# Layer 1's scores computed for two heads at a time, from keys and queries that are no longer stacked

## The chip, the core and the metric

The kernel runs on one core of a Trainium2 chip. TensorE multiplies matrices out of SBUF into PSUM, VectorE (DVE), ScalarE (ACT) and GpSimd (POOL) do the elementwise work, and SyncE (SP) issues nearly all DMAs, which share 16 DMA engines. The metric is the device time of one execution in microseconds. Before the change three runs took 1598.06, 1599.79 and 1607.69 us, with a median of 1599.79 us.

## The reference

Two layers of cross attention work on 8 batches. Each batch has 100 queries and a context of 722 rows, all 512 wide. Layer 0 has 16 heads of 32 features, layer norms and a feed forward of 2048. Layer 1, cut to what matters here, is:

```python
qh = (q @ Wq).reshape(b, sq, H, DK)            # H = 16 heads, DK = 64
kh = (k @ Wk).reshape(b, sk, H, DK)            # sk = 722
vh = (v @ Wv).reshape(b, sk, H, DV)
attn = jnp.einsum('bqhd,bkhd->bhqk', qh / jnp.sqrt(jnp.float32(DK)), kh)
weights = jax.nn.softmax(attn + gaussian_w, axis=-1)
out = jnp.einsum('bhqk,bkhd->bqhd', weights, vh).reshape(b, sq, H * DV)
out = layernorm(out @ Wfc + residual)
```

A score is thus a sum over 64 features, while TensorE's array has 128 rows to sum over.

## The kernel before, in words

Float32 numbers are kept as pairs of float16, a high part and a low part, and a product of two such pairs is made of the terms high·high, high·low and low·high (`TERMS`), summed in PSUM.

The work goes by 24 units. Units 0 to 7 are layer 0, one batch each, with 16 heads. Units 8 to 23 are layer 1: a unit is half of a batch's heads, so 8 heads of 64 features. While the heads of one unit are worked on, the keys and values of the next unit are projected (`proj`), and between them run the feed forward, the queries of layer 1 and the output projections.

**Keys.** `proj_k` makes 4 pieces of 128 features (two heads of layer 1) by two halves of 361 keys. Each half is 12 matmuls into a PSUM bank; ACT writes the high part (`nc.scalar.copy`) and DVE the low part into a tile `KN` (2 buffers) whose 128 partitions are the features of two heads. When both halves are done, `stack` makes layer 1's stacked form in a tile of `KSR` (4 tiles, 4 heads each, tile name `ks`): per head, 64 partitions with the high part and 64 with the low part. That takes four DMAs per piece, from SBUF to SBUF. `keys_free` holds back the piece that takes the next `KSR` tile until the heads that last used that tile are on their way.

**Queries.** The queries of layer 1 lie in DRAM (`QD1`). `load_q` brings them in with four DMAs per unit, high and low parts each twice, once for each half of the partitions.

**Scores.** `scores` makes, for one head and each half of 361 keys, two matmuls with 128 rows: the high query part against high and low keys stacked, then the low query part against the same. (So low·low is included.) The result is a tile `S` of two PSUM banks; the pool `ps_s` has two such tiles. DVE takes the maximum over the 722 keys (`nm`). `front1` then scales it (`nb`), makes the exponentials on ACT (`p`), casts them to float16 (`stage`, by ACT or DVE in turns), makes the low part on POOL, and transposes both with a DMA into a tile `pt`. `head_back` multiplies `pt` with `V` in 18 matmuls into `O`.

**What sets the order.** `step(u, h)` writes the scores of head h and then the softmax of the head before it, which waited in `stages`. Between the steps the fill items (`merge`) are written at even rates, each with a cost by hand. In layer 1 `nc.in_order` is empty: the order on each engine is chosen at build time by a planner that simulates the engines and takes, of what is ready, the instruction that stands earliest in the program. Everything in `step` counts as standing 120 instructions earlier than it is written (80 in the last unit). So a head's four score matmuls are planned as single instructions among those of other streams, and need not stay together.

PSUM has 8 banks: 4 for the two `S` tiles, 1 for `O`, and 3 for all projections (`pp` twice and `nzb`).

Of the kernel before, what the change touches and what calls it, by code (L numbers as in the profile page):

```python
# [21 lines left out]
# the products of a split pair: high*high, high*low, low*high  # L22
TERMS = ((0, 0), (0, 1), (1, 0))
# layer 0's rows of outputs: the heads whose products share a bank of PSUM
# [4 lines left out]
class Engine:  # L29
    """an engine whose instructions can be kept in the order in which they are written"""  # L30
# [23 lines left out]
def xattn_kernel(  # L54
# [33 lines left out]
    # resident weights: what layer 0 is done with makes room for layer 1  # L88
# [56 lines left out]
    def pow2_steps(s, inv, u, k, n):  # L145
        """s = 2**e with sqrt(u) * s <= 2**(15 - k), inv = 1 / s"""
        t, t2, V = small(n, I32, "pa"), small(n, I32, "pb"), nc.vector
        return [
            lambda: V.tensor_single_scalar(t, u.bitcast(I32), 1, ALU.logical_shift_right),
            lambda: V.tensor_scalar(t2, t, -1, 0x5F30F379, ALU.mult, ALU.add),  # L150
            lambda: V.tensor_single_scalar(t, t2, 0x7F800000, ALU.bitwise_and),
            lambda: V.tensor_scalar(s, t.bitcast(F32), 2.0 ** (15 - k), None, ALU.mult),
            lambda: V.tensor_scalar(inv.bitcast(I32), s.bitcast(I32), -1, 254 << 23, ALU.mult, ALU.add)]
# [5 lines left out]
    def rsqrt_steps(v, eps, n, p=128, scale=1.0):  # L159
        """scale / sqrt(v + eps), by Newton's method: the steps and the result"""  # L160
        a, i, yi = small(n, tag="ra"), small(n, I32, "ri"), small(n, I32, "ry")
        V = nc.vector
        l = [lambda: V.tensor_scalar(a[:p], v, eps, None, ALU.add),
             lambda: V.tensor_single_scalar(i[:p], a[:p].bitcast(I32), 1, ALU.logical_shift_right),
             lambda: V.tensor_scalar(yi[:p], i[:p], -1, 0x5F3759DF, ALU.mult, ALU.add),
             lambda: V.tensor_scalar(a[:p], a[:p], -0.5, None, ALU.mult)]
        y = yi.bitcast(F32)
        for it in range(3):
            t, y2 = small(n, tag="rt"), small(n, tag="rz")
            if n == 1:  # L170
                l.append(lambda t=t, y=y: V.tensor_scalar(t[:p], y[:p], y[:p], a[:p], ALU.mult, ALU.mult))
            else:
                l += [lambda t=t, y=y: V.tensor_tensor(t[:p], y[:p], y[:p], ALU.mult),
                      lambda t=t: V.tensor_tensor(t[:p], t[:p], a[:p], ALU.mult)]
            l.append(lambda t=t, y=y, y2=y2: V.scalar_tensor_tensor(y2[:p], t[:p], 1.5, y[:p], ALU.add, ALU.mult))
            y = y2
        if scale != 1.0:
            l.append(lambda: V.tensor_scalar(y[:p], y[:p], scale, None, ALU.mult))
        return l, y
# [7 lines left out]
    def colsum(src, n, p=128):  # L187
        """sums over the partitions, on every partition, in PSUM"""
        ps = psum_misc()
        nc.tensor.matmul(out=ps[:, :n], lhsT=ones[:p, :], rhs=src, start=True, stop=True)  # L190
        return ps[:, :n]
# [8 lines left out]
    XS = 4.0  # scale of what a layer norm returns: at most sqrt(512)  # L200

# [1 line left out]
    # blocks of 256 columns or 256 rows, each with its scale and the inverse; wo has one scale  # L203
# [3 lines left out]
    def weighted_rows(raw, c, acc):  # L207
        """sum over kc of raw[:, kc, :] * c[:, kc], by partition"""
        nc.vector.tensor_scalar(acc, raw[:, 0, :], c[:, 0:1], None, ALU.mult)
        for kc in range(1, KC):  # L210
            nc.vector.scalar_tensor_tensor(acc, raw[:, kc, :], c[:, kc : kc + 1], acc, ALU.mult, ALU.add)
        return acc

    def bias_part(ps, raw, bcol, ocs):
        """ps[:, oc] = sum over rows of raw[row, oc] * bcol[row]"""
# [6 lines left out]
    # -- layer 0: wq, wk, wv, with the gain and shift of the layer norm folded in  # L222
# [30 lines left out]
    # |g| + |b|: with it the sum of squares of a weight bounds what its product with a normed row, shift  # L253
    # included, can be
# [31 lines left out]
    def scale_steps(i, name):  # L286
        """the scale of a weight of layer 0"""
# [26 lines left out]
    # -- DRAM scratch  # L314
# [76 lines left out]
    def first_load():  # L391
        """the context of batch 0, the queries of batches 0 and 1, the weights of layer 0"""
# [81 lines left out]
    def v_tile(u, s):  # L474
        """V of half the heads of a unit: [lo | hi | 1] by head in layer 0, [hi | lo] in layer 1"""
# [11 lines left out]
    def proj_v0(u):  # L487
        L, b, hf = unit_of(u)

        def pair(s, c):  # L490
            """two chunks of keys for half the heads"""
# [52 lines left out]
    def load_q(u, oc=None):  # L544
# [9 lines left out]
        else:  # L554
            q = pool.tile([128, 16, SQ], F16, tag="QS", name="QS").rearrange("p (t h) q -> p t h q", t=2)
            src = QD1.rearrange("(g d) t k -> d g t k", d=64)
            for r in range(2):
                for t in range(2):
                    nc.sync.dma_start(
                        out=q[64 * r : 64 * r + 64, t],  # L560
                        in_=src[:, 8 * hf : 8 * hf + 8, t, b * SQ : (b + 1) * SQ])
# [5 lines left out]
    def keys_free():  # L567
        """whether the heads that use the next tile for a stack of keys are all on their way"""
        return owner.get(counters.get("ks", 0) % len(KSR), None) in used | {None}
# [6 lines left out]
    def proj_k(u):  # L576
# [3 lines left out]
        def piece(oc, j):  # L580
            w = w0["k"] if L == 0 else w1res["k", hf]
            T = ctxT[L, b]
            if j == 0:
                kn[oc] = pool.tile([128, 2, SK], F16, tag="KN", name="KN", bufs=2)
# [18 lines left out]
        def stack(oc):  # L603
# [8 lines left out]
            else:  # L612
                if oc % 2 == 0:
                    KSt[u, oc // 2] = keys_tile(u, 2 * oc + 3)
                KS = KSt[u, oc // 2]
                for j in range(2):
                    for t in range(2):
                        nc.sync.dma_start(
                            out=KS[64 * t : 64 * t + 64, 2 * (oc % 2) + j, :SK], in_=K[64 * j : 64 * j + 64, t, :])
            if u > 0 and oc == (1 if u == LAST else 2 if u < B else 3):  # L620
                load_q(u)
        def item(oc, j):
            f = lambda: piece(oc, j)
            if j == 1 and (L == 0 or oc % 2 == 0):
                f.ready = keys_free
# [8 lines left out]
    def scores(u, h):  # L634
# [3 lines left out]
        for j in range(2):  # L638
            sl = slice(j * HALF, (j + 1) * HALF)
            if L == 0:  # L640
                nc.tensor.matmul(
                    out=S[:SQ, j, :HALF], lhsT=q[:96, h, :], rhs=KS[:96, h % 4, sl], start=True, stop=True)
            else:
                for t in range(2):
                    nc.tensor.matmul(
                        out=S[:SQ, j, :HALF], lhsT=q[:, t, h, :], rhs=KS[:, h % 4, sl], start=(t == 0), stop=(t == 1))
        nm = small(1, tag="nm")
        nc.vector.tensor_reduce(nm[:SQ], S[:SQ, :, :HALF], AX.XY, ALU.max, negate=True)
        return S, nm

    # layer 0: the scores again with the keys on the partitions, less the maximum of each query, which
    # enters the product as two more rows (a power of two by a split pair)
# [105 lines left out]
    def to_T(src, dst, s=None):  # L758
        """split [100, 512] and transpose it into dst [128, 8, 112]"""
# [12 lines left out]
    def o_transposed(u, half=None):  # L772
# [4 lines left out]
        else:  # L777
            # chunks in the order hi 0, hi 1, lo 0, lo 1 | hi 2, hi 3, lo 2, lo 3
# [8 lines left out]
    def project_out(u_list, scr):  # L787
        """[100, 512] = concatenation of the units' outputs times a streamed weight"""
# [152 lines left out]
    ahead = {}  # L941

    def load_ahead():
        """what the ends of the last two batches read"""
# [8 lines left out]
    def out_row(b, ap):  # L953
        """gamma or beta on every partition"""
# [22 lines left out]
    usum = const.tile([128, 8], F32, name="usum")  # L977

    def pipeline(blocks):
        """the steps of the blocks, in an order in which each has the next ones' behind it"""  # L980
# [10 lines left out]
    def block(w, kind, i, col, scr=None, dst=None, total=None, done=None):  # L991
        """kind "rows": rows 256 i up; "cols": columns 256 i up"""
# [70 lines left out]
    def y_scale():  # L1063
        """sy = (scale of what the feed forward's layer norm returns, its inverse, bound of the sum of its squares)"""
# [106 lines left out]
    def merge(lists):  # L1171
        """one list in which the given lists advance at even rates"""
# [224 lines left out]
    def step(u=None, h=None):  # L1397
        """one head further: scores of the next, softmax of the one before, output of an earlier one"""
        with tc.high_priority(offset=80 if u == LAST or u is None and len(pending) and pending[0][0] >= LAST - 1 else 120):
            new = None  # L1400
            if u is not None:
                S, nm = scores(u, h)
                new = (u, h, S, negated(nm) if u < B else nm)
                if u < B:
                    negated_T(u, h, new[3])
# [4 lines left out]
            if new:  # L1410
                stages.append(new)
# [84 lines left out]
```

## Time and profile before

| | |
|---|---|
| runs, us | 1598.06, 1599.79, 1607.69 |
| profiled execution: span, us | 1602.2 (the page gives no other time for it) |
| mean granted TensorE clock | 0.948 of full speed |
| layer 1's part, first score matmul to the end | 712.4 us to 1602.2 us |
| PE busy, whole span | 1390.2 us, 87% |
| DVE, ACT, POOL busy | 66%, 50%, 38% |
| DMA queue of SP | 77.6% of 16 engines' span |

Nearly all instructions carry line L39, that of the helper `Engine.__getattr__` which records every operation. So groups are told apart by their tiles, written as out<-in, with the engine ahead: "PE S<-ks,QS" are the score matmuls, "ACT KN<-pp" the high parts of keys. PEld is the load of a matmul's stationary operand, which overlaps PE. A form such as 128\*100 gives the rows and columns of the array that a matmul uses; 128x361 behind it is what streams through. "busy" is the union of a group's time, then comes the mean duration of one, and then the idle time of the engine just before it with what ended it.

### The profile page before, as it was taken

What the parts mean: (1) busy time and instruction counts of PE and PEld (TensorE: products, weight loads), DVE (VectorE), ACT (ScalarE), POOL (GpSimd) and SP (SyncE); (2) the same over time, 40 slices, a digit from 0 to 9 for tenths busy, and PEclk for the clock granted to TensorE, in tenths of its full rate; (3) what the DMA queues carried; (4) which work ended last, traced back from release to release, by engine and by line L of the source; (5) the groups of instructions that cost most, each with busy time, mean ns of one, the idle gap of its engine ahead of it and who ended that gap; (6) DMA issues with size and microseconds to landing.
All of it is one profiled execution on the core that took longest, in us unless ns stands there. A gap on an engine that the chain in (4) does not pass through costs nothing. (4 is left out here: it accounts for less than half of the span.)

```text
span 1602.2 us, 33216 instructions
## 1 busy us (share of the span) xinstructions
PE 1390.2 (87%) x12394; PEld 973.7 (61%) x12394; DVE 1062.2 (66%) x2761; ACT 797.2 (50%) x1518; POOL 606.0 (38%) x465
## 2 busy tenths in 40 slices
PE   5887888788877989787999889999979999889996
PEld 4665566666656666465666556566556666565674
DVE  6878788888898576785455655455745455545566
ACT  3455656776765566644444334444424443343442
POOL 3234565766764244453222213222313222223341
PEclk9899899898878999999999999999999999999999
DMA  8567789778975595569987689988888976797675
GB/s 200 128 138 182 166 239 207 194 211 199 253 156 137 159 233 169 157 168 187 209 175 176 164 184 205 214 181 176 193 158 200 218 179 168 163 189 161 156 170 112
DMA packets 504019, 289.71 MB, mean 181 GB/s; under 512 B 397054, under 2 KB 435982, under 8 KB 503858
## 3 DMA queue, kind: packets, MB, share of 16 engines
q1 hardware_dynamic: 501714, 287.58, 77.6%
q8 instruction: 97, 1.59, 0.4%
q14 instruction: 64, 0.52, 0.1%
q10 hardware_dynamic: 2112, 0.01, 0.1%
q0 software_dynamic: 32, 0.01, 0.0%
HBM read 149.37 MB, written 35.30 MB: 115 GB/s over the span
## 5 line engine op out<-in xcount | busy, mean ns | idle before, releaser
L39 POOL TENSOR_TENSOR stage<-p,stage 100x722 f16<-100x722 f32 x124 | 196.8, 1590 | 526.4 <-DVE stage L39 250.2
L39 PE MATMUL pp<-wres,ctxT 128*128 128x256 f16 (+3 forms) x1992 | 340.3, 323 | 17.6 <-DVE V L39 12.2
L39 PE MATMUL pp<-ctxT,wres 128*128 128x361 f16 x1800 | 328.0, 332 | 15.0 <-DVE QN L39 6.2
L39 PEld LDWEIGHTS <-wres 128*128 128x128 f16 x2496 | 244.9, 102 | 153.7 <-issue 39.1
L39 PEld LDWEIGHTS <-ctxT 128*128 128x128 f16 (+1 forms) x2376 | 240.9, 105 | 152.1 <-issue 22.1
L39 DVE TENSOR_REDUCE nm<-S 100x1 f32<-100x722 f32 x256 | 229.9, 900 | 67.2 <-PE S L39 66.3
L39 POOL TENSOR_TENSOR pt<-p,pt 128x600 f16<-128x600 f32 x128 | 177.0, 1385 | 168.7 <-ACT pt L39 117.6
L39 PE MATMUL O<-V,pt 128*128 128x64 f16 (+5 forms) x3840 | 193.8, 192 | 28.8 <-DMA pt<-stage 11.2
L39 PEld LDWEIGHTS <-pt 128*128 128x128 f16 (+1 forms) x3840 | 170.6, 99 | 70.6 <-DMA pt<-stage 14.7
L39 PE MATMUL S<-ks,QS 128*100 128x361 f16 (+1 forms) x768 | 186.0, 330 | 30.2 <-issue 8.0
L39 ACT ACTIVATE p<-S,nb,sig 100x722 f32<-100x722 f32 x128 | 121.9, 953 | 156.8 <-DVE nb L39 138.7
L39 ACT CAST V<-pp 128x256 f16<-128x256 f32 (+2 forms) x194 | 78.3, 406 | 121.9 <-DVE V L39 57.4
L39 DVE TENSOR_TENSOR V<-pp,V 128x256 f16<-128x256 f32 (+2 forms) x194 | 89.6, 463 | 63.6 <-ACT V L39 63.4
L39 PEld LDWEIGHTS <-QS 128*100 128x100 f16 (+1 forms) x768 | 91.7, 129 | 61.5 <-issue 29.9
L39 PEld LDWEIGHTS <-wst 128*128 128x128 f16 x1152 | 101.5, 100 | 23.8 <-issue 12.7
L39 ACT ACTIVATE p<-ST,sig 128x600 f32<-128x600 f32 x128 | 97.4, 761 | 27.2 <-PE ST L39 22.7
L39 PE MATMUL nzb<-ctxT,wres 128*128 128x361 f16 x504 | 90.0, 324 | 6.5 <-DVE V L39 2.9
L39 ACT CAST pt<-p 128x600 f16<-128x600 f32 x128 | 87.9, 688 | 2.3
L39 PE MATMUL nzb<-wres,ctxT 128*128 128x512 f16 (+2 forms) x384 | 88.5, 373 | 0.2 <-DVE V L39 0.2
L39 DVE SCALAR_TENSOR_TENSOR hl<-nat,sc,hl 128x512 f16<-128x512 f32 (+1 forms) x48 | 40.8, 851 | 63.5 <-ACT hl L39 63.4
L39 DVE TENSOR_TENSOR KN<-pp,KN 128x361 f16<-128x361 f32 x86 | 45.3, 530 | 54.2 <-ACT KN L39 53.4
L39 PE MATMUL pp<-wst,hT 128*100 128x512 f16 x312 | 76.4, 380 | 2.0 <-DMA wst<-W2S 0.9
(259 smaller groups left out, 2065.6 us busy)
## 6 DMA issues: line engine op xcount, KB each, us to landing
ks<-KN SPq DMA_DIRECT2D x256, 90.2 KB
nat<-in_ctx_dram SPq DMA_DIRECT2D x78, 256.0 KB
ks<-KD SPq DMA_DIRECT2D x96, 180.5 KB
wst<-W1S SPq DMA_DIRECT2D x64, 256.0 KB
wst<-W2S SPq DMA_DIRECT2D x64, 256.0 KB
wst<-WFS SPq DMA_DIRECT2D x48, 256.0 KB
KD<-KN SPq DMA_DIRECT2D x32, 361.0 KB
QS<-QD SPq DMA_DIRECT2D x85, 100.0 KB
```

Of the source, the lines that this page charges most:

```text
L39: r = f(*args, **kwargs)
```

## The change

Layer 1's keys are written by ACT and DVE straight into the `KSR` tile, with the partitions as they come out of the projection: partitions 0 to 63 are one head, 64 to 127 the next, and high and low parts lie side by side. The four stacking DMAs per piece go. Queries are loaded the same way, with two DMAs per unit. The new `scores_pair` makes the scores of two heads together: three terms instead of two stacked products, each a matmul over 64 rows, the first head on rows 0 to 63 and the second on rows 64 to 127, written in turn. It is called at even heads, and takes both `S` tiles. The product low·low is no longer computed. `step` now writes the softmax of the waiting head before the scores. Layer 0 is as before.

```diff
@@ load_q
-            q = pool.tile([128, 16, SQ], F16, tag="QS", name="QS").rearrange("p (t h) q -> p t h q", t=2)
-            src = QD1.rearrange("(g d) t k -> d g t k", d=64)
-            for r in range(2):
-                for t in range(2):
-                    nc.sync.dma_start(
-                        out=q[64 * r : 64 * r + 64, t],
-                        in_=src[:, 8 * hf : 8 * hf + 8, t, b * SQ : (b + 1) * SQ])
+            q = pool.tile([128, 16, SQ], F16, tag="QS", name="QS")[:, :8].rearrange("p (c t) q -> p c t q", t=2)
+            src = QD1.rearrange("(c p) t k -> p c t k", p=128)
+            for t in range(2):
+                nc.sync.dma_start(out=q[:, :, t], in_=src[:, 4 * hf : 4 * hf + 4, t, b * SQ : (b + 1) * SQ])
@@ proj_k, piece
             if j == 0:
-                kn[oc] = pool.tile([128, 2, SK], F16, tag="KN", name="KN", bufs=2)
+                if L == 0:
+                    kn[oc] = pool.tile([128, 2, SK], F16, tag="KN", name="KN", bufs=2)
+                else:
+                    if oc % 2 == 0:
+                        KSt[u, oc // 2] = keys_tile(u, 2 * oc + 3)
+                    kn[oc] = KSt[u, oc // 2][:, 2 * (oc % 2) : 2 * (oc % 2) + 2, :SK]
@@ proj_k, stack and item
-            else:
-                if oc % 2 == 0:
-                    KSt[u, oc // 2] = keys_tile(u, 2 * oc + 3)
-                KS = KSt[u, oc // 2]
-                for j in range(2):
-                    for t in range(2):
-                        nc.sync.dma_start(
-                            out=KS[64 * t : 64 * t + 64, 2 * (oc % 2) + j, :SK], in_=K[64 * j : 64 * j + 64, t, :])
...
-            if j == 1 and (L == 0 or oc % 2 == 0):
+            if j == 1 if L == 0 else j == 0 and oc % 2 == 0:
                 f.ready = keys_free
@@ scores
-            if L == 0:
-                nc.tensor.matmul(
-                    out=S[:SQ, j, :HALF], lhsT=q[:96, h, :], rhs=KS[:96, h % 4, sl], start=True, stop=True)
-            else:
-                for t in range(2):
-                    nc.tensor.matmul(
-                        out=S[:SQ, j, :HALF], lhsT=q[:, t, h, :], rhs=KS[:, h % 4, sl], start=(t == 0), stop=(t == 1))
+            nc.tensor.matmul(
+                out=S[:SQ, j, :HALF], lhsT=q[:96, h, :], rhs=KS[:96, h % 4, sl], start=True, stop=True)
+        return S, maximum(S)
...
+    def scores_pair(u, h):
+        S = [ps_s.tile([128, 2, 512], F32, tag="S", name="S") for _ in range(2)]
+        K, q = KSt[u, h // 4][:, h % 4 : h % 4 + 2], QSt[u]
+        for j in range(2):
+            sl = slice(j * HALF, (j + 1) * HALF)
+            for i, (a, t) in enumerate(TERMS):
+                for r in range(2):
+                    rows = slice(64 * r, 64 * r + 64)
+                    nc.tensor.matmul(
+                        out=S[r][:SQ, j, :HALF], lhsT=q[rows, h // 2, a, :], rhs=K[rows, t, sl],
+                        start=(i == 0), stop=(i == 2))
+        return [(s, maximum(s)) for s in S]
@@ step
-            new = None
-            if u is not None:
+            new = []
+            if u is not None and u < B:
                 S, nm = scores(u, h)
-                new = (u, h, S, negated(nm) if u < B else nm)
-                if u < B:
-                    negated_T(u, h, new[3])
+                new = [(u, h, S, negated(nm))]
+                negated_T(u, h, new[0][3])
             if len(stages) >= (2 if u is not None and u < B else 1):
                 v, g, S_, nm_ = stages.pop(0)
                 pending.append((v, g, front0(v, g, nm_) if v < B else front1(v, g, S_, nm_)))
                 used.add((v, g))
-            if new:
-                stages.append(new)
+            if u is not None and u >= B and h % 2 == 0:
+                new = [(u, h + r, S, nm) for r, (S, nm) in enumerate(scores_pair(u, h))]
+            stages.extend(new)
```

`maximum` is the old code's reduction to `nm`, now a function of its own.

More of the change, by code (lines that the diff above doesn't have):

```diff
@@ L639, in scores, with maximum @@
             sl = slice(j * HALF, (j + 1) * HALF)
-            if L == 0:
-                nc.tensor.matmul(
-                    out=S[:SQ, j, :HALF], lhsT=q[:96, h, :], rhs=KS[:96, h % 4, sl], start=True, stop=True)
-            else:
-                for t in range(2):
-                    nc.tensor.matmul(
-                        out=S[:SQ, j, :HALF], lhsT=q[:, t, h, :], rhs=KS[:, h % 4, sl], start=(t == 0), stop=(t == 1))
+            nc.tensor.matmul(
+                out=S[:SQ, j, :HALF], lhsT=q[:96, h, :], rhs=KS[:96, h % 4, sl], start=True, stop=True)
+        return S, maximum(S)
+    def maximum(S):
         nm = small(1, tag="nm")
         nc.vector.tensor_reduce(nm[:SQ], S[:SQ, :, :HALF], AX.XY, ALU.max, negate=True)
-        return S, nm
+        return nm
+    def scores_pair(u, h):
[10 more added lines that the diff above has]
+        return [(s, maximum(s)) for s in S]
     def negated(nm):
```

## The prediction

> **What bounds the kernel now.** I read the page's busy shares first, then the busy time by stretches, then the groups by form inside layer 1's stretch, then the matmuls in order of time. The first line is the page's, the next two the view by stretches:
>
> ```profile
> PE 1390.2 (87%) x12394; PEld 973.7 (61%) x12394; DVE 1062.2 (66%) x2761; ACT 797.2 (50%) x1518; POOL 606.0 (38%) x465
> ...
> core 0: us, PE busy (x) PEld busy (x) DVE busy (x) ACT busy (x) POOL busy (x), PEclk, DMA share, GB/s
> 712.00:1602.00 890.00, 815.14 (x6824) 535.08 (x6824) 499.47 (x1141) 368.29 (x731) 240.60 (x160) 0.98 0.82 179
> ```
>
> In layer 1 PE is busy 815 of 890 us; the DMA engines come second with 0.82, while DVE and ACT have room. What a change does to PE's stream is therefore nearly what it does to the time. The groups by form, in 712 to 1602 us:
>
> ```profile
> L39 PE MATMUL S<-ks,QS 128*100 128x361 f16 x512 | 119.6, 326 | 13.5 <-issue 8.0 <-DMA ks<-KN 3.4 <-ACT p L39 2.0
> L39 DVE TENSOR_REDUCE nm<-S 100x1 f32<-100x722 f32 x128 | 115.0, 901 | 42.2 <-PE S L39 42.0
> L39 PEld LDWEIGHTS <-wst 128*128 128x128 f16 x900 | 78.1, 99 | 16.4 <-issue 7.1 <-DVE V L39 2.2 <-DVE QN L39 1.4
> L39 PEld LDWEIGHTS <-QS 128*100 128x100 f16 x512 | 63.4, 127 | 39.5 <-issue 12.9 <-DMA ks<-KN 2.4 <-DMA xs<-in_L_xattn_beta_dram 0.7
> L39 ACT CAST KN<-nzb 128x361 f16<-128x361 f32 x42 | 19.3, 460 | 52.9 <-PE nzb L39 32.8 <-DMA ks<-KN 20.1
> ```
>
> A matmul's duration is not its price, since the next starts before it ends. The timeline of PE gives the price, and also shows how the score matmuls of one head stand among the others (two heads here):
>
> ```profile
> 1009.13 0.79 PE L39 MATMUL S<-ks,QS 128*100 128x361 f16 x4 [0.40 <-DMA ks<-KN]
> ...
> 1430.94 0.33 PE L39 MATMUL S<-ks,QS 128*100 128x361 f16 x1 [1.14 <-DMA ks<-KN]
> 1431.11 0.32 PE L39 MATMUL pp<-ctxT,wres 128*128 128x361 f16 x1
> 1431.26 0.32 PE L39 MATMUL S<-ks,QS 128*100 128x361 f16 x1
> 1431.41 0.32 PE L39 MATMUL pp<-ctxT,wres 128*128 128x361 f16 x1
> 1431.57 0.32 PE L39 MATMUL S<-ks,QS 128*100 128x361 f16 x1
> 1431.72 0.32 PE L39 MATMUL pp<-ctxT,wres 128*128 128x361 f16 x1
> 1431.88 0.32 PE L39 MATMUL S<-ks,QS 128*100 128x361 f16 x1
> ```
>
> Four matmuls in 0.79 us, the last of which takes 0.32, start 0.154 to 0.157 us apart: 361 columns cost 0.154. The second head is what matters most here: its matmuls alternate with a projection's. I went through all 128 heads of layer 1 in this view: in 56 the four stand together, in 60 two or three of the three links between them are broken, mostly by one foreign matmul each time. Today that is free, as 0.154 is kept throughout.
>
> **The sum, against the profiled execution's span of 1602.2 us.** The median is 2.4 us lower, inside the runs' spread, so differences are carried over to 1599.8.
>
> *Streams.* Before, two heads take 8 x 0.154 = 1.232 us; 64 pairs are 78.8 us. After, there are 12 matmuls of the same 361 columns. Where both halves of the rows really work at once, the six slots cost 6 x 0.154 = 0.924 us, so 59.1 us in all, a gain of 19.7. Where every matmul runs alone, 12 x 0.154 x 64 = 118.3 us, a loss of 39.5. No matmul of the trace uses half the rows, so these are the bounds. Two matmuls can only run at once if they are neighbours. The two chains of a pair are written in turn and should be ready together (the waits are below), so whole bursts come in the right order, but a stream that stands at the same place in the plan cuts in between. Of the bursts I take 60/128 = 47% as cut. A cut lasts as long as the other chain: 12 or 18 matmuls, entered half way on average, so some 7 of a burst's 11 links. With the odd single cut that is 3.6 broken links per burst, one in three. Six slots then cost 6 x 0.154 x 1.33 = 1.23 us: **0 us**, the gain is eaten by the cuts.
>
> *Changes between half rows and whole rows.* A burst with 3.6 cuts is 4.6 runs, each entered and left: 9.2 changes, 64 x 9.2 = 590. The trace has none, so its price is bounded. Below: nothing, as changes between 96, 98 and 128 rows cost nothing visible. Above: the new matmul waits until the one before has left the array, 0.317 (the median duration of a score matmul) less 0.154 = 0.163 us. I take 0.10, which is nearest to the row of weight loads (99 ns): what today hides beneath the preceding matmul would stand free once per change. That is **+59 us**; the bounds are 0 and +96.
>
> The Trainium skill, "TensorEngine Tiling (Array Packing)", section Tiling Modes (Key Properties), speaks against this change: going from one tiling mode to another, not merely to another tile, drains the engine. No row here shows that; by it the price would lie nearer to the whole tail of a matmul, and the sum nearer to its upper bound. Against that, "TensorE: Matmul & The Clock Gate", Part 3 (Measured speedup vs the span model) gives row tiles that start some 4 ns apart, by which an uncut burst gains nearly all of what the two halves can give; no row here shows that either.
>
> *Weight loads.* 768 in place of 512, 127 ns each as 100 columns; the matmul before hides one. Two per slot, 0.254 us of durations, overlap each other as today's loads do: 0 where they still do so. If they didn't, six slots would lose 0.1 us each, 38 us, no more than the bound of matmuls that run alone.
>
> *DMAs that go.* 256 of 90.2 KB, of which the tile's view shows SP's issue cost:
>
> ```profile
> L39 SPq DMA_DIRECT2D ks<-KN x252: 461/587/1863, 703.6 to 1568.0; - x126
> ```
>
> 252 x 0.587 = 148 us of SP's queue, and by the packet records (15,868 of 1444 bytes, 95 ns each, on 16 engines) 94 us of the engines' 890: their share falls from 0.82 to 0.71. The queries' DMAs fall from 64 to 32. None of it is on the path by itself; the path has PE's idle time that a DMA ended: 27.2 us in layer 1 (`pt` 11.2, `wst` 9.0, `ks` 3.4, `OT` 2.0, smaller ones 1.6). Shorter queues take back a part, between 0 and 27: **-10 us**, the 3.4 and a quarter of the rest. ACT's 29 us of waiting for a free `KN` buffer (20.1 in the last row above) go too, but ACT is idle half the time.
>
> *New waits.* The pair needs both `S` tiles, so its first matmuls stand behind the exponentials of the two heads before; queued behind them on PE is everything else. A pair comes every 890/64 = 13.9 us, and after its scores come two maxima (0.90 each), `nb` (0.24) and two exponentials (0.95 and 0.19 for the sum): some 4.3 us. So 0, with 9 us of cover; without it, up to 4.3 us a pair. DVE's two maxima in a row hold up what stands behind them, the low parts of V and K, by 0.9 us; PE has three banks for projections, and waits 23 us for DVE in layer 1 today. 0, at most 0.9 x 64 = 58 if each delay reached PE. Keys now wait for a free `ks` tile one piece earlier; its last readers are a unit back: 0.
>
> Sum: 0 + 59 - 10 = +49, so **1649 us**.
>
> **The rivals.**
>
> *Faster: the halves work at once and changing costs little.* -19.7 - 10 = -30, **1570 us**, if bursts stay whole and changes are free. For it: 56 of 128 heads stand together today, and both chains of a pair can fill each other's gaps. Against it: the 60 that don't. It decides when streams and changes together cost less than the 10 us from the DMAs: with uncut bursts (128 changes) below 0.23 us a change, with today's cuts below 0.017.
>
> *A wash.* Cuts as today, changes free: 0 - 10, **1590 us**. For it: mixing row counts is free today.
>
> *The halves don't run side by side* (the change doesn't do what it says): +39.5 - 10 = +29, **1629 us**. For it: no matmul of the trace overlaps another's streaming.
>
> *Changing costs the whole tail*: +96 - 10 = +86, **1686 us**.
>
> **Chances and range.** Cut bursts with a change of about a weight load: 0.42. Faster: 0.22. Wash: 0.13. Side by side fails: 0.12. Whole tail, or more cuts than today: 0.11. A measurement of this kernel tells about 1%, 16 us, from no change. That makes 0.22 faster, 0.13 within 1%, 0.65 slower. Cases of both signs hold most of the chance, so the range goes from the faster rival, with some of the DMAs' upper bound, 1566, to the whole tail with part of the two maxima's cost, 1715. The likeliest case's own range is 1612 to 1686.
>
> **What the changed profile would show.** Score matmuls of form 64\*100, 768 of them, whose starts come two at a time if the halves work at once, and 0.154 us apart if not. In the timeline, single score matmuls between foreign ones if the cuts stay, and starts more than 0.154 after a matmul of the other row count if changing costs. No `ks<-KN`, a DMA share near 0.71, PE's idle time behind DMAs below 27 us. "DVE nm" twice in a row, and "PE S" still hardly waiting for "ACT p". I would be wrong if the planner kept bursts whole, or if a change were free; and too low if a weight load could not begin before the array is empty.

## The result: slower by 3.6%, and where the time went

The changed kernel takes 1659.1 us (median of 4 runs, 1651.88 to 1671.47) against 1600.3 us before (median of 4). The ratio is 1.0363, with a 95% interval of 1.0325 to 1.0401. The profiled execution has a span of 1661.8 us, 59.6 us above that of before. Layer 1, from its first score matmul to the end, grew from 889.8 to 948.3 us, by 58.5; so nearly all of it lies there.

The lines that answer to those of before are these: first the page's busy shares, then busy time in layer 1's stretch, then three groups by form in the same stretch.

```profile
PE 1486.2 (89%) x12650; PEld 979.4 (59%) x12650; DVE 1071.5 (64%) x2761; ACT 791.0 (48%) x1518; POOL 606.5 (36%) x465
```

```profile
core 0: us, PE busy (x) PEld busy (x) DVE busy (x) ACT busy (x) POOL busy (x), PEclk, DMA share, GB/s
713.00:1662.00 949.00, 915.20 (x7128) 543.89 (x7125) 508.69 (x1150) 364.22 (x733) 244.28 (x164) 0.98 0.64 140
```

```profile
L39 PE MATMUL S<-ks,QS 64*100 64x361 f16 x768 | 169.1, 339 | 2.7 <-DMA QS<-QD 1.4 <-ACT p L39 1.2
L39 PE MATMUL O<-V,pt 128*128 128x64 f16 x1920 | 110.1, 194 | 5.5 <-DMA pt<-stage 5.5
L39 ACT CAST ks<-pp 128x361 f16<-128x361 f32 x81 | 37.4, 461 | 123.3 <-PE pp L39 123.2
```

PE is busy 96% of layer 1 where it was 92%, and the DMA engines went from 0.82 to 0.64. The score matmuls have the form 64\*100 now, so they do use half the rows. ACT's writing of keys, which had waited 29 us for the stacking DMAs to free `KN`, now waits for nothing but PE. "ACT p" holds up a score matmul for 1.2 us in all: that the pair needs both `S` tiles costs next to nothing.

The timeline of PE shows the price. First a pair that nothing cut, then a stretch of one that was cut at every link:

```profile
958.91 1.14 PE L39 MATMUL S<-ks,QS 64*100 64x361 f16 x12 [0.80 <-DMA QS<-QD]
959.99 0.33 PE L39 MATMUL nzb<-ctxT,wres 128*128 128x361 f16 x1
960.15 0.69 PE L39 MATMUL O<-V,pt 128*128 128x64 f16 x18
...
1534.17 0.28 PE L39 MATMUL O<-V,pt 128*128 128x64 f16 x4
1534.38 0.35 PE L39 MATMUL S<-ks,QS 64*100 64x361 f16 x1
1534.67 0.20 PE L39 MATMUL O<-V,pt 128*128 128x64 f16 x1
1534.80 0.35 PE L39 MATMUL S<-ks,QS 64*100 64x361 f16 x1
1535.09 0.20 PE L39 MATMUL O<-V,pt 128*128 128x64 f16 x1
1535.22 0.35 PE L39 MATMUL S<-ks,QS 64*100 64x361 f16 x1
1535.50 0.20 PE L39 MATMUL O<-V,pt 128*128 128x64 f16 x1
```

Uncut, twelve matmuls take 1.14 us, the last one's end included, and 1.08 from the first start to the next matmul's. At 0.154 each they would take 1.85 to that point: the two halves do work at once. Cut, one score matmul and one `O` matmul take 0.42 us (1534.38 to 1534.80), where whole rows would take 0.154 + 0.029 = 0.18. So a way there and back costs 0.24 us.

Over all of layer 1, from the start-to-start times of PE's 7,100 matmuls (a step is compared with the usual step after a matmul of that width; steps that exceed it by more than 0.4 us are counted as waits):

| us of layer 1 | before | after | |
|---|---|---|---|
| score matmuls, streaming | 81 | 93 | +12 |
| changes between half and whole rows | 3 | 89 | +86 |
| waits of PE | 70 | 27 | -43 |
| all the rest | 736 | 739 | +3 |

The kernel before has no half rows, so its 3 us of changes are what this way of counting leaves over. The score matmuls of the changed kernel stand in 392 runs, so there are 784 changes at 0.114 us: entering half rows costs 0.10 us, leaving them 0.13 on average (0.13 after a run of one or two matmuls, 0.09 after a longer one). A slot is the place of one matmul of each head: of 384 slots 178 overlap. And 43 us of PE's waits have gone, for which the prediction had 10. The experiments take these three apart.

### The profile page after: what moved, and what is told of

Same layout as the page of the kernel before. It is cut to its first block, busy times and chain, and to the rows that moved or that the text cites. A ratio compares the mean times of both kernels' runs of the same rounds, so it can differ in the third digit from the quotient of the medians.

```text
span 1661.8 us, 33017 instructions
## 1 busy us (share of the span) xinstructions
PE 1486.2 (89%) x12650; PEld 979.4 (59%) x12650; DVE 1071.5 (64%) x2761; ACT 791.0 (48%) x1518; POOL 606.5 (36%) x465
## 4 chain that ended last, share of the span: by engine, by line
PE 41%; DMA 6%; DVE 3%; issue 2%; POOL 1%; SPq 1%; ACT 1%; POOLq 0%; ACTq 0%; DVEq 0%
PE pp L39 21%; PE nzb L39 9%; PE S L39 7%; PE O L39 4%; DMA wst<-WFS 2%; SPq L39 1%; DMA xs<-in_L_xattn_gamma_dram 1%; DMA ctxT<-hl 1%; POOL stage L39 1%; DVE hl L39 1%; POOL xs L39 1%; DMA OT<-hl 0%; ACT p L39 0%; DVE nm L39 0%; DMA xs<-X 0%
## 5 line engine op out<-in xcount | busy, mean ns | idle before, releaser
L39 PE MATMUL pp<-wres,ctxT 128*128 128x256 f16 (+3 forms) x1992 | 350.6, 329 | 11.9 <-DVE V L39 7.3
L39 PE MATMUL pp<-ctxT,wres 128*128 128x361 f16 x1800 | 334.8, 333 | 17.0 <-DVE QN L39 6.4
L39 PE MATMUL S<-ks,QS 64*100 64x361 f16 (+1 forms) x1024 | 235.9, 339 | 18.9 <-DVE nm L39 7.4
L39 POOL TENSOR_TENSOR pt<-p,pt 128x600 f16<-128x600 f32 x128 | 173.1, 1355 | 176.3 <-ACT pt L39 115.9
L39 PE MATMUL O<-V,pt 128*128 128x64 f16 (+5 forms) x3840 | 202.0, 192 | 24.0 <-DVE ut L39 6.8
L39 PEld LDWEIGHTS <-QS 64*100 64x100 f16 (+1 forms) x1024 | 94.0, 123 | 84.1 <-issue 61.1
L39 ACT CAST ks<-pp 128x361 f16<-128x361 f32 x86 | 39.7, 461 | 128.0 <-PE pp L39 127.0
L39 POOL TENSOR_SCALAR stage<-stage,SC 128x512 f32<-128x512 f32 x32 | 56.8, 1775 | 54.6 <-ACT whl L39 20.1
```

What stands on the lines that cost most here:

```text
L39: r = f(*args, **kwargs)
```

## The experiments

The theory: PE pays for every change between half and whole rows, and the bursts, as planned, are cut often. The rivals: changes are free, and the loss is that of twelve matmuls in place of eight; or the overlap is worth nothing. A second question is whether the 43 us came from the DMAs that went, or were only hidden behind a longer stream. All comparisons below are with the kernel before on the same chip, which took 1605.3 us there.

**Bursts kept whole.** All twelve matmuls get the same place in the plan and are kept in the order in which they are written:

```diff
+                    with tc.high_priority(offset=6 * j + 2 * i + r):
                         nc.tensor.matmul(
                             out=S[r][:SQ, j, :HALF], lhsT=q[rows, h // 2, a, :], rhs=K[rows, t, sl],
                             start=(i == 0), stop=(i == 2))
+                    nc.in_order = ("tensor",)
+        nc.in_order = ()
```

> The changed kernel, with the twelve score matmuls of a pair given one place in the plan and kept in the order in which they are written, so that other streams cut in rarely: 111 runs of score matmuls in place of 392, 222 changes between half and whole rows in place of 784. Theory (changes cost PE time, and cuts lose the overlap of the two halves): 562 changes fewer at 0.113 us are -64 us, and some 150 slots more that overlap are -23 us; a part of the idle time that the longer stream hid comes back, some +20. About 1592 us, 1575 to 1615. Rival (changes are free, the time went into twelve matmuls in place of eight that don't overlap when cut): only the -23 us, about 1636 us.

Measured: 1589.9 us, a ratio of 0.9906 (0.9871 to 0.9941). This version is faster than both kernels, and 0.9% faster than the one before. In its timeline and its layer 1:

```profile
804.85 0.25 PE L39 MATMUL O<-V,pt 128*128 128x64 f16 x3
805.03 1.13 PE L39 MATMUL S<-ks,QS 64*100 64x361 f16 x12
806.09 0.58 PE L39 MATMUL O<-V,pt 128*128 128x64 f16 x14
```

```profile
718.00:1589.00 871.00, 813.92 (x7118) 510.92 (x7118) 506.99 (x1149) 362.85 (x732) 251.67 (x164) 0.99 0.69 153
```

The steps between the twelve starts of this burst are, in ns (the starts at even places belong to the other half of the rows):

```
3 189 4 150 3 150 3 155 3 149 3      then 247 to the next matmul over whole rows
```

Two matmuls start 3 or 4 ns apart and each such slot costs 0.15 us, but the first 0.19, and leaving costs 0.09 more. Changes now cost 23 us in place of 89, streaming 67 in place of 93, and 349 of 384 slots overlap. The rival without a price for changes had 1636 us; it falls. But streams and changes together are 90 us, where the kernel before has 84; what else makes this version faster is looked at below.

**The same order, but whole rows.** The cuts stay as in the changed kernel, instruction for instruction on PE; only the rows differ:

```diff
-                    rows = slice(64 * r, 64 * r + 64)
+                    rows = slice(0, 128)
```

> The changed kernel with every matmul of a pair over all 128 rows, in the same order on PE, cuts included. It leaves out the separation of the two heads: each score is summed over both heads' features. No change between half and whole rows is left, and no overlap. Theory (changes cost): -89 us for the changes, +25 us for the 178 slots that overlapped, some +15 us of idle time that comes back: about 1610 us, 1595 to 1630. Rival (changes are free): 1659 + 25 = 1684 us.

Measured: 1605.7 us, a ratio of 0.9995 (0.9970 to 1.0021). Without half rows the very same order of twelve matmuls takes 3.7% less of the time of before than with them (0.9995 against 1.0363). The 89 us of changes are gone and no slot overlaps.

**Whole rows and whole bursts.** Both edits together.

> wide_rows with the order of whole_bursts: every matmul over all 128 rows (each score summed over both heads' features), bursts cut in 111 runs in place of 392. If cuts cost something by themselves, for instance since the maximum of a head comes later: 10 us or more below wide_rows. Theory (cuts cost only by the changes of rows and the lost overlap, and here is neither): as wide_rows, within 5 us.

Measured: 1610.3 us, 1.0027 (1.0000 to 1.0054), as wide_rows or 5 us more. Cuts by themselves cost nothing that can be seen; on half rows the same difference in order is worth 4.6%.

**The kernel before with whole bursts**, its four matmuls kept together in the same manner:

```diff
+                    with tc.high_priority(offset=None if (j, t) != (0, 0) else 0):
                         nc.tensor.matmul(
                             out=S[:SQ, j, :HALF], lhsT=q[:, t, h, :], rhs=KS[:, h % 4, sl], start=(t == 0), stop=(t == 1))
+                    nc.in_order = ("tensor",)
+        nc.in_order = () if L else nc.in_order
```

> The kernel before with the four score matmuls of a head kept together: 127 runs in place of 293. Theory: changes nothing, 0.995 to 1.005 of the kernel before. Rival (whole bursts win by themselves, whatever the rows): 0.99 or less.

Measured: 1610.4 us, 1.0030 (1.0009 to 1.0050). Nothing is won, so the gain of whole_bursts isn't that of a better order as such.

**The DMAs alone.** The kernel before with the new keys and queries, and its own scores, read from the unstacked tiles:

```diff
-                        out=S[:SQ, j, :HALF], lhsT=q[:, t, h, :], rhs=KS[:, h % 4, sl], start=(t == 0), stop=(t == 1))
+                        out=S[:SQ, j, :HALF], lhsT=q[:, h // 2, t, :], rhs=KS[:, h % 4 // 2 * 2 + t, sl],
+                        start=(t == 0), stop=(t == 1))
```

> The kernel before with unstacked keys and queries, and its old scores of one head at a time, two matmuls over 128 rows for each half of the keys. It leaves out the separation of the heads (each score is summed over both heads' features) and the mixed products of high and low parts. TensorE's work is that of before; only the stacking DMAs and their waits are gone. If their going is worth the 10 us of the prediction: about 1590 us. If it is what took 43 us of idle time out of layer 1: about 1557 us. If the idle time was only hidden behind the longer stream: 1600 us.

Measured: 1586.1 us, 0.9879 (0.9842 to 0.9916): 19 us, between the 10 and the 43. In layer 1:

```profile
716.00:1584.00 868.00, 812.67 (x6862) 535.74 (x6862) 512.65 (x1150) 369.38 (x732) 246.47 (x164) 0.98 0.69 153
```

PE is busy 812.7 us, as before (815.1); the stretch is 22 us shorter. PE's waits by the steps are 48 us, where they were 70. Of those that the view by form gives a cause, the ones ended by DMAs fell by only 6 us, from 27.2 to 21.4; those put down to "issue" fell from 8.0 to 0, by ACT from 5.6 to 1.6 and by DVE from 23.4 to 21.4. All of the 8.0 had stood just before score matmuls, whose group is now

```profile
L39 PE MATMUL S<-ks,QS 128*100 128x361 f16 x512 | 125.4, 322 | 5.1 <-DMA QS<-QD 4.3 <-ACT p L39 0.6 <-DVE ks L39 0.2
```

**The DMAs kept.** The changed kernel that issues them still, into tiles that nobody reads:

```diff
+            if L == 1:
+                for j in range(2):
+                    spare = pool.tile([128, 2, SK], F16, tag="KN", name="KN", bufs=2)
+                    for t in range(2):
+                        nc.sync.dma_start(out=spare[64 * t : 64 * t + 64, 0], in_=K[64 * j : 64 * j + 64, t, :])
```

> The changed kernel that still issues the four stacking DMAs per piece of keys, into tiles that nobody reads. If the DMAs' going is worth 10 us: about 1669 us. If it is worth the 43 us of idle time: about 1700 us. If nothing: 1659 us.

Measured: 1683.1 us, 1.0484 (1.0451 to 1.0516), so 1.2% of the time of before, some 19 us, above the changed kernel's 1.0363, give or take 8. So by the medians both directions give the DMAs' going some 19 us. The profiles agree less well: layer 1 is 22 us shorter without the DMAs, and 11 us longer with them kept, 959.1 us in place of 948.3. No score waits for the kept ones, and the longer stream can hide more. The score matmuls have 392 runs here too, and the changes cost 90 us.

So of the 43 us of waits about half, 19 to 22, went with the DMAs. The other 21 to 24 were hidden behind the longer stream: PE's waits are 48 us in no_stacking_dmas and 27 in the changed kernel, neither of which has the DMAs. wide_rows and no_stacking_dmas show it without any change of rows: the one has 4 x 64 matmuls more, 39.5 us of PE, and takes only 19.6 us longer.

```profile
713.00:1602.00 889.00, 847.07 (x7118) 564.69 (x7116) 511.14 (x1150) 362.37 (x732) 243.61 (x164) 0.99 0.68 150
```

This is wide_rows: PE is 34 us busier than in no_stacking_dmas, and the stretch is 21 us longer. PE's waits fell from 48 to 35 us; the likely reason is that the same transfers and PSUM evacuations have more PE work beside them.

**The two heads one after the other.** One place in the plan, but no order among the twelve: the planner then puts the six of the first head before the six of the second (34 of 64 bursts are exactly so).

```diff
+                    with tc.high_priority(offset=6 * j + 2 * i + r):
                         nc.tensor.matmul(
```

> The changed kernel with the matmuls of a pair at one place in the plan but no order among them: 104 runs, and the six of the first head stand before the six of the second, so that neighbours mostly use the same half of the rows. 208 changes, about as in whole_bursts, but hardly any overlap. Theory (the two halves at once are worth 0.15 us per slot): some 275 slots that no longer overlap are +41 us against whole_bursts, less some 10 us of idle time that they hide: about 1.010 of the kernel before, 1.002 to 1.018. Rival (overlap is worth nothing since weight loads or PSUM bound the slots): as whole_bursts, 0.991.

Measured: 1604.0 us, 0.9992 (0.9968 to 1.0015). The overlap that is lost is worth 0.9% against whole_bursts, so the rival falls; but the loss is 14 us where 31 were expected. The timeline shows a burst:

```profile
743.72 1.48 PE L39 MATMUL S<-ks,QS 64*100 64x361 f16 x12
745.12 0.26 PE L39 MATMUL O<-V,pt 82*128 82x64 f16 x3
```

That is 1.48 us, not the 2.0 of twelve matmuls one by one. TensorE doesn't keep to the program's order here: see the last section. Streaming costs 90 us of layer 1, 23 more than in whole_bursts and not 41; changes are 2.5 us less and PE's waits 5.

**Still fewer cuts.** All but the first matmul of a pair stand at the front of the plan:

```diff
-                    with tc.high_priority(offset=6 * j + 2 * i + r):
+                    with tc.high_priority(offset=None if (j, i, r) != (0, 0, 0) else 0):
```

> As whole_bursts, but all matmuls of a pair after its first stand at the very front of the plan: 92 runs of score matmuls in place of 111, 184 changes between half and whole rows in place of 222, some 10 more slots that overlap. Theory (changes and lost overlap cost): 38 changes fewer at 0.113 us and 10 slots at 0.15 us are -6 us against whole_bursts, so about 0.987 of the kernel before, 0.980 to 0.993. Rival (what whole_bursts won came from the DMAs alone and the last changes don't matter): as whole_bursts, 0.991.

Measured: 1595.7 us, 0.9939 (0.9915 to 0.9962), which whole_bursts' interval overlaps, and above the 0.980 to 0.993 expected. The changes did get cheaper, 18 us in place of 23, but PE's waits came to 61 us, where they are 49 in whole_bursts. Why they grew wasn't followed up.

## Why the prediction was right, step by step

The forecast was 1649 us and slower; 1659 was measured. The mechanism of the likeliest case held, and its three terms were each off, in ways that nearly cancelled: streams and changes were 39 us too low together, what PE would wait less 33 us too low. That the sum came within 10 us is luck.

- *Streams: 0 forecast, +12 measured.* The two bounds were right, since overlapping slots do cost 0.15 us. But I took two thirds of the slots as overlapping, 256 of 384, and 178 did. That only neighbours can run at once was too strict, as the last section shows.
- *Changes: +59 forecast, +86 measured.* The number of cuts was the larger error: 4.6 runs per burst were forecast and 6.1 found, 784 changes in place of 590. How long a cut burst is cut was about right: 48 bursts had two links or more broken, 6.7 on average, where 7 were forecast. Their share was wrong, 48 of 64 in place of 47%: it was read from single heads, and a burst holds two. If each of the two is cut with 47%, 72% of the bursts are. The price, 0.10 taken, was 0.114, within the bounds. The reason given for it did not hold: no weight load stands free ahead of the matmul. After the uncut burst above the load begins at 959.985 us and its matmul at 959.989; what costs is a pause of 0.09 us before both, and that it is about as long as a load is luck.
- *DMAs: -10 forecast, -43 of waits measured.* Two things were mixed up here. The DMAs' going is worth 19 us. The 6 us that went of the waits ended by DMAs are near the quarter that was taken; what the sum put at nothing are the other waits that went with them, 8 us of "issue" before score matmuls, 4 of ACT and 2 of DVE by the profile of no_stacking_dmas. And the sum let every us of added PE work through to the end. Some 21 to 24 us of other waits lay beside that work and vanished under it.
- *New waits and weight loads, forecast at 0, were about 0.* PE waited 1.2 us for the exponentials; 6.2 us for DVE, where it had been 23.4.

The Trainium skill's rule, "TensorEngine Tiling (Array Packing)", section Tiling Modes (Key Properties), that changing the mode drains the engine, fits the trace: the last score matmul of the uncut burst above starts at 959.742 us, so its streaming ends at 959.896 by 0.154, and no weight load over whole rows begins before 959.985, where such loads otherwise run during the matmul before. The price that the prediction drew from it, the whole tail of 0.163, would have been too high: 0.10 and 0.13 were measured.

The faster rival was rightly stated, with its condition. whole_bursts meets that condition, as its streams and changes cost 6 us more than before, less than the DMAs bring; it is faster, by 15 us and not by 30. Even an uncut burst pays for its entry, its exit and a first slot of 0.19 us. It takes 1.06 us to the next matmul and 0.10 to enter, so 1.16 against 1.23 for two heads before: a gain of 5 us if all 64 pairs were uncut, and 29 are. The DMAs alone brought 19 us in no_stacking_dmas, which is no slower than whole_bursts (1586.1 against 1589.9 us, with intervals that overlap). So all that whole_bursts wins can be the DMAs', and no run here shows a gain of the pairing itself over the stacked scores.

## What to carry to other kernels

Two matmuls on the two halves of TensorE's rows do run at once, but each change between half and whole rows costs about 0.11 us in this kernel. So such matmuls must be long or many, and stand together; where a planner orders single instructions, they have to be tied together by hand. When work is added to a bound engine that still waits now and then, only part of it shows in the time, here half (39.5 us added, 19.6 seen) to four fifths (100 us more in streams and changes from no_stacking_dmas to the changed kernel, 4.8% or 78 us seen); when a DMA is taken away, run that alone to see what it was worth.

## What the runs showed of the hardware that was not expected

TensorE took matmuls out of order between the two halves of its rows. In whole_one_by_one, where the six matmuls of the first head stand in the program before the six of the second, the starts of one burst are as follows, in us. The marks come from the semaphores: "waits" is on the first matmul of a head, "tells" on its last.

```
743.716 waits   743.908   744.062   744.068 waits   744.215   744.260
744.373         744.413   744.525 tells  744.567    744.724   744.877 tells
```

The second head's first matmul starts at 744.068, ahead of three of the first head's, of which the last starts at 744.525. From then on the two heads' matmuls run beside each other. All 34 bursts that stand in the program in this order start in the same pattern, within 3 ns. The Trainium skill, "TensorE: Matmul & The Clock Gate", Part 3 (The mechanism), has matmuls start and end in strict program order; here they did not, and the measurement decides. So part of the overlap comes without writing the two halves in turn, if they stand close enough: 110 slots started together within 30 ns, and others shared part of their time.

The weight load of 100 columns was not in the way. In whole_bursts, where 349 of 384 slots overlap, 768 loads of 122 ns each lay mostly beneath slots of 0.15 us, two at a time:

```profile
L39 PEld LDWEIGHTS <-QS 64*100 64x100 f16 x768 | 44.5, 122 | 39.6 <-issue 25.0 <-DMA QS<-QD 6.6 <-PE nzb L39 0.2
```
